# Layer 0 of a two-layer kernel: token buffers in two pairs, bias adds moved to block 3, no direct sums in block 6, the first block's own pieces in one step

## The chip, the cores and the metric

The kernel runs on one core of one Trainium2 chip. The metric is device time in microseconds (us), the median of several runs. The profile is of one execution, taken by the hardware profiler. Its engines are PE (TensorE; PEld are its weight loads), DVE (VectorE), ACT (ScalarE), POOL (GpSimd) and SP (SyncE, which here issues most DMAs). L1421 is line 1421 of the kernel before.

## The reference, cut to what matters

Two layers work on 4096 tokens of 256 features, all in float32. Layer 0, which the change touches, is attention over all tokens:

```python
x = layernorm(h); q = x @ wq.T + bq + sym_emb            # h: 32 x 128 tokens, 256 features
Q, K, V = q @ wQ.T + bQ, h @ wK.T + bK, h @ wV.T + bV     # 8 heads of 32
scores = einsum(Q, K) / sqrt(32)
scores = where(t_key > t_query, -inf, scores)             # t: time of the token, 0..127
ctx = softmax(scores) @ V
h = h + alpha * (ctx @ out_w.T + out_b)
```

Layer 1 is attention in a window of 24 tokens and then eight experts of three matrices each, weighted by a router. The change leaves it as it is.

## The kernel before

Layer 0 works on **8 blocks** of 512 tokens, sorted by time, so that block b sees the keys of blocks 0 to b alone. The 8 heads are two groups of four. A **unit** (b, g) is one block of queries with one group of heads; it is cut into **steps**, one for each tile of 128 keys (4b + 3 steps for group 0, 4b + 2 for group 1; the last tiles of a unit, which are partly masked, share steps). 265 steps in all are issued one after the other by one Python loop (from L1576). For each engine this order is the program, since the schedule is written out by hand. In pass n of the loop:

- `scores` (L1330): PE multiplies queries and keys of step n. The first head goes to the PSUM tile `sa` (one buffer), the other three to `sb` (two buffers, pool `ps_b`). Projections and sums take their PSUM from `ps_b` too, through `banks`.
- `product` (L1421): PE adds the weights times the values of step n - 2 to `av`. When a unit ends here, `evacuate` (L1436) copies `av` out on ACT, between the two exponentials.
- `exps`: ACT takes the exponential of `sa` (L1343) and of `sb` (L1345) into a tile `pt` (five buffers). Where a step crosses the mask, POOL clears corners of `pt` by three memsets (L1357); DVE and PE read `pt` after these.
- `add` (L1371 to L1407): DVE adds the `pt` of step n - 1 to `acc`, two heads at a time. This is for the sum of each softmax row.
- `close_sums` (L1451): one pass after the last product of a unit, PE adds up `acc` over the key partitions. Steps listed in `direct` are left out by `add`, and their `pt` is summed by PE here. `direct` held one step of either unit of block 6 and two of either unit of block 7.
- `invert` and `scale` (L1490, L1503), five and eleven passes later: the sums go through DRAM by small DMAs (`r16`, `flat`, `rec`) and DVE multiplies `ctx` by the inverse.
- Between these, `prep(b + 1)` makes the next block's keys, values and queries in four pieces: transposes (L986), keys (L995), values (L1041), queries (L1014). The loop spreads `count` pieces evenly over the block's steps. In block 0, the pieces of `rest_of_first` go ahead of them: the values of block 0, then keys and queries of its group 1. The pieces of `output_weights` (block 2) and `expert_norms` (block 3) come behind `prep`; the latter issue the copy `bnT` on DVE (L1265) and the band mask `bandb` on POOL (from L1237).

Input tiles come by DMAs on SP's queue, in the order of issue: `load_x` (L946) loads a block sorted by time ("xg" for projections, "xs" for the statistics of the layer norm), and `load_tokens` (L898) loads a block in its plain order ("tokens"), for the residual sum in layer 1's first part. All take buffers of 512 KB from the pool `tok`: one ring of four, tag "xg". A buffer is handed on when its last reader is done. `send_rstd(b + 1)` (L974, L978) sends the next block's inverse deviations through DRAM into a tile `rb`; it is issued on SP at the second step of a block, ahead of tokens that are loaded at the third.

`with_bias(n)` (L906) adds the output bias `outb` (made in block 2) to token tile n, on POOL. Tiles 0 to 11 were done in layer 0, six in the second unit of block 5 and six in that of block 6; the rest later. POOL runs its instructions in order and waits only for data, so an add that is written in a step may run as soon as the instruction ahead of it on POOL is done.

Of the kernel before, what the change touches and what calls it, by code (L numbers as in the profile page):

```python
# [10 lines left out]
F32 = mybir.dt.float32  # L11
# [5 lines left out]
P = 128  # L17
# [806 lines left out]
def fast_kernel(ctx: ExitStack, tc: tile.TileContext, ins: dict, out: bass.AP, narrow):  # L824
    nc = tc.nc
    x = ins["x"]
    _, N, T, D = x.shape
# [5 lines left out]
    NBLK = NT // BLK  # L833
    TPB = BLK // P
    HG = P // HD
    NGRP = H // HG
# [8 lines left out]
    def row(ap):  # L845
        return ap.rearrange("(o d) -> o d", o=1)
# [43 lines left out]
        nc.gpsimd.memset(big_t[:, :, z : z + SIDE], 0.0)  # L890


    tok = ctx.enter_context(tc.tile_pool(name="tok", bufs=4))
    held_tokens = {}

    def load_tokens(b, t):
        held_tokens[b] = t
        nc.sync.dma_start(  # L898
            out=t, in_=x[0, b * TPB : (b + 1) * TPB].rearrange("n t d -> t n d")
        )  # L900

    def tokens(n):
        return held_tokens[n // TPB][:, n % TPB, :]

    def with_bias(n):
        nc.gpsimd.tensor_tensor(tokens(n), tokens(n), outb, op=ALU.add)  # L906
# [21 lines left out]
    with ExitStack() as l0:  # L928
# [7 lines left out]
        rblk = {}  # L936

        def load_x(b, name, amid=()):
            xg = tok.tile([P, TPB, D], F32, tag="xg", name=f"{name}{b}")
            for tl in range(TT):  # L940
                if tl < len(amid):
                    amid[tl]()
                src = x[0][:, b * TPB * TT : (b + 1) * TPB * TT, :].rearrange(
                    "n (i tl) d -> tl n i d", tl=TT
                )[tl]
                nc.sync.dma_start(out=xg[tl * N : (tl + 1) * N], in_=src)  # L946
            return xg
# [140 lines left out]
        with tc.tile_pool(name="pw", bufs=1) as pw, tc.tile_pool(  # L1088
            name="ptr", bufs=8, space=PSUM
# [112 lines left out]

        def output_weights(banks):

            wo_n = tok.tile([P, TPB, D], F32, tag="xg", name="wo_n")[:, :2, :]
            nc.sync.dma_start(
                out=wo_n, in_=ins["L0_conv_out_w"].rearrange("(c p) d -> p c d", p=P)
            )
            nc.sync.dma_start(out=alpha, in_=row(ins["L0_conv_alpha"]).to_broadcast([P, 1]))
            nc.sync.dma_start(out=outb, in_=row(ins["L0_conv_out_b"]).to_broadcast([P, D]))  # L1210
            bvb = px.tile([P, 2, P], F32, tag="bvb", name="bvb", bufs=1)
            for c in range(2):
                nc.vector.tensor_copy(bvb[:, c, :], colT[:, c, 6:7].to_broadcast([P, P]))
            yield
            pss = banks("ps_wo", 2)
            for c in range(2):
                for k in range(2):
                    nc.tensor.transpose(
                        pss[c][:, k * P : (k + 1) * P], wo_n[:, k, c * P : (c + 1) * P], ident
                    )  # L1220
            for c in range(2):
                nc.scalar.copy(woT[:, c, :], pss[c][:, :D])
            nc.vector.tensor_scalar(woT, woT, alpha, None, op0=ALU.mult)
            yield
            ps = banks("ps_ob", 1)[0][:, :D]
            for c in range(2):
                nc.tensor.matmul(
                    ps, lhsT=bvb[:, c, :], rhs=woT[:, c, :], start=(c == 0), stop=(c == 1)
                )
            nc.vector.scalar_tensor_tensor(  # L1230
                out=outb, in0=outb, scalar=alpha, in1=ps, op0=ALU.mult, op1=ALU.add
            )
            yield
# [36 lines left out]
        with ExitStack() as at:  # L1270
# [29 lines left out]
            units = {(b, g): unit_steps(b, g) for b in range(NBLK) for g in range(NGRP)}  # L1300
            steps = [(b, g, k) for (b, g), unit in units.items() for k in range(len(unit))]

            direct = {u: () for u in units}
            for b, count in ((NBLK - 2, 1), (NBLK - 1, 2)):
                last = len(units[b, 0]) - 1
                direct[b, 0] = tuple(range(last - 1, last - 1 + count))
                last = len(units[b, 1]) - 1
                direct[b, 1] = tuple(range(last + 1 - count, last + 1))

            def carried(b, g):  # L1310

# [127 lines left out]
            FIRST = 3 * TPB  # L1439
# [96 lines left out]
            for n in range(10):  # L1536
                count = 3 if n < 4 else 2
# [19 lines left out]
            def rest_of_first():  # L1557
                pss = banks("psv0", 2)
                for f in [project_v(0, i2, hT0, pss[i2], True) for i2 in range(TPB // 2)]:
                    f()  # L1560
                yield
                for g in range(1, NGRP):
                    pss = banks(f"pskq0_{g}", 2)
                    copies = (
                        project_k(0, g, hT0, pss[0], True),
                        project_q(0, g, hT0, pss[1], later=True),
                    )
                    for f in copies:
                        f()
                    yield  # L1570


            u, z = NBLK - 3, NBLK - 2
            tokens_at = [(u, 0, 2), (u, 0, 4), (u, 1, 0), (z, 1, 0)]
            todo, done, count = iter(()), 0, 0
            later = {}  # L1576
            for n in range(len(steps) + LAG + 1 + 16):
                if n < len(steps):
                    b, g, k = steps[n]
                    own = sum(len(units[b, i]) for i in range(NGRP))  # L1580
                    if g == 0 and k == 0:
                        for _ in todo:
                            pass
                        todo, done, count = iter(()), 0, 5
                        if b + 1 < NBLK:
                            todo = prep(b + 1, banks)
                            if not b:
                                send_rstd(1)
                        if b == 0:
                            todo, count = itertools.chain(rest_of_first(), todo), 8  # L1590
                        if b == 2:
                            more = output_weights(banks)
                            next(more)
                            todo, count = itertools.chain(todo, more), 7
                        if b == 3:
                            more = expert_norms(banks)
                            next(more)
                            todo, count = itertools.chain(todo, more), 6
                        if 2 <= b < NBLK - 2:
                            xblk[b + 2] = load_x(b + 2, "xg")  # L1600
                    scores(b, g, k)
# [23 lines left out]
                if n < len(steps):  # L1625
                    at_step = g * len(units[b, 0]) + k + 1
                    closing = any(f is close_sums for f, _ in later.get(n, []))
                    if due == 2:
                        invert_rstd()
                        due = 0  # L1630
                    while done < count * at_step // own and not (closing and b):
                        if due == 1:

                            root_rstd()
                            due = 2
                        next(todo, None)
                        done += 1
                    if (b, g, k) in tokens_at:
                        nb = tokens_at.index((b, g, k))
                        load_tokens(  # L1640
                            nb, tok.tile([P, TPB, D], F32, tag="xg", name=f"tokens{nb}")
                        )
                    if n in load_at:
                        for lb in load_at[n][1:]:
                            got = xstat if load_at[n][0] == "xs" else xblk
                            got[lb] = load_x(lb, load_at[n][0])
                    for sb_, si in stat_at.get(n, ()):
                        stats(sb_, si, xstat[sb_])
                        if (sb_, si) == (NBLK - 1, TPB - 1):
                            cols = slice(2 * TPB, NTILE)  # L1650
                            nc.vector.tensor_scalar(
                                rstd0[:, cols], mean0[:, cols, 1], 1e-5, None, op0=ALU.add
                            )
                            due = 1
                    if 1 < b < NBLK - 1 and not g and k == 1:
                        send_rstd(b + 1)
                    if NBLK - 3 <= b < NBLK - 1 and g and 4 <= k < 4 + FIRST // 2:
                        with_bias((b - NBLK + 3) * FIRST // 2 + k - 4)
                for f, u in later.pop(n, []):
                    f(*u)  # L1660

# [838 lines left out]
    for name, cost, f, needs in jobs:  # L2500
        own = isinstance(name, tuple) and isinstance(name[1], int)
        b = name[1] if own else 2
        if own and name[0] in ("project", "normalise", "turn"):
            b = max(1, (b - 1) // TPB)
# [47 lines left out]
    for k in range(len(work)):  # L2552
# [7 lines left out]
        if k + 1 < len(work):  # L2560
            nb = work[k + 1][0]
# [23 lines left out]
        if one:  # L2585
            name = f"th{k + 1}"
# [55 lines left out]
```

## Time and profile before

| what | us |
|---|---|
| median of 3 runs (lowest, highest) | 1478.73 (1478.14, 1479.79) |
| profiled execution | 1477.89 |
| its span | 1476.1 |
| layer 0's steps, first to last exponential | 19.64 to 694.67 |
| block 3, unit 0 / unit 1, from | 155.03 / 196.68 |
| block 5, unit 1, from | 381.32 |
| block 6, unit 0 / unit 1, from | 436.05 / 499.42 |
| block 7, unit 0 / unit 1, from | 563.46 / 630.53 |

A unit starts here where ACT starts its first exponential. Granted clock of PE: 1.00 in all these stretches.

A row of the timeline has the start, the busy time of the merged instructions, engine, line, operation, tile written and tiles read, shape, count, and in brackets how long the engine stood idle before and what ended that. SPq rows are DMAs being issued, not transferred. A row of groups has count, busy time and mean. Idle time of an engine costs time only if the engine is the bound there, or if one that is waits for it.

### The profile page before, as it was taken

What the parts mean: (1) busy time and instruction counts of PE and PEld (TensorE: products, weight loads), DVE (VectorE), ACT (ScalarE), POOL (GpSimd) and SP (SyncE); (2) the same over time, 40 slices, a digit from 0 to 9 for tenths busy, and PEclk for the clock granted to TensorE, in tenths of its full rate; (3) what the DMA queues carried; (4) which work ended last, traced back from release to release, by engine and by line L of the source; (5) the groups of instructions that cost most, each with busy time, mean ns of one, the idle gap of its engine ahead of it and who ended that gap; (6) DMA issues with size and microseconds to landing.
All of it is one profiled execution on the core that took longest, in us unless ns stands there. A gap on an engine that the chain in (4) does not pass through costs nothing.

```text
span 1476.1 us, 23637 instructions
## 1 busy us (share of the span) xinstructions
PE 1454.4 (99%) x8873; PEld 842.4 (57%) x8873; DVE 1198.8 (81%) x2189; ACT 936.6 (63%) x1357; POOL 153.1 (10%) x318
## 2 busy tenths in 40 slices
PE   9999999999999999999899999999999999999998
PEld 6433232322322322222567888888888888888887
DVE  4778989899999999999647777777777778777775
ACT  4777878888889889988464445445445544444443
POOL 2211011000200200000163013020011000000000
PEclk9999999999999999999999999999999999999999
DMA  6220101021000000000332333433334344334442
GB/s 137 52 56 9 40 1 37 1 44 38 2 15 23 1 9 9 1 9 20 101 134 96 110 120 123 132 121 110 122 111 127 116 127 130 108 122 127 130 150 67
DMA packets 96377, 110.15 MB, mean 75 GB/s; under 512 B 17949, under 2 KB 85232, under 8 KB 96256
## 3 DMA queue, kind: packets, MB, share of 16 engines
q1 hardware_dynamic: 93280, 106.87, 24.3%
q8 instruction: 72, 1.18, 0.3%
q0 software_dynamic: 1888, 0.91, 0.2%
q10 hardware_dynamic: 1088, 0.79, 0.2%
q14 instruction: 49, 0.40, 0.1%
HBM read 98.87 MB, written 8.53 MB: 73 GB/s over the span
## 4 chain that ended last, share of the span: by engine, by line
PE 82%; DVE 10%; issue 3%; ACT 3%; DMA 1%; SPq 0%; DVEq 0%; POOL 0%; ACTq 0%; POOLq 0%
PE psh L2082 22%; PE sa L1330 14%; PE av L1421 14%; PE psy L2148 13%; DVE acc L1407 3%; PE psv L1041 2%; PE psk L995 2%; PE psq L1014 2%; PE psk L1831 2%; PE sums L1451 1%; PE sb L1330 1%; ACT h L2065 1%; PE psh L2087 1%; PE pso L1516 1%; PE pss L1843 1%
## 5 line engine op out<-in xcount | busy, mean ns | idle before, releaser
L1407 DVE TENSOR_TENSOR acc<-acc,pt 128x1024 f32<-128x1024 f32 (+2 forms) x470 | 517.7, 1167 | 22.0 <-POOL pt L1357 11.1
L1345 ACT ACTIVATE pt<-sb 128x1536 f32<-128x1536 f32 (+1 forms) x265 | 382.8, 1445 | 3.0 <-PE sb L1330 2.9
L1330 PE MATMUL sb<-q,kT 32*128 32x512 f32 (+3 forms) x1728 | 299.8, 600 | 0.5 <-DVE bnT L1265 0.5
L1330 PE MATMUL sa<-q,kT 32*128 32x512 f32 (+3 forms) x576 | 296.5, 600 | 1.9 <-ACT pt L1343 0.7
L2065 ACT ACTIVATE h<-h,bshift,bscale 128x256 f32<-128x256 f32 x244 | 159.2, 699 | 214.4 <-DVE h L2124 214.3
L1421 PE MATMUL av<-pt,v 128*32 128x512 f32 (+3 forms) x2304 | 281.4, 568 | 0.6
L2148 PE MATMUL psy<-wo,h 128*128 128x256 f32 x1024 | 243.6, 381 | 0.0
L2148 PEld LDWEIGHTS psy<-wo,h 128*128 128x128 f32 x1024 | 191.5, 190 | 31.0 <-issue 5.5
L1330 PEld LDWEIGHTS sa<-q,kT 32*128 32x128 f32 x576 | 85.8, 183 | 205.8 <-ACT pt L1343 171.6
L1343 ACT ACTIVATE pt<-sa 128x512 f32<-128x512 f32 (+1 forms) x265 | 157.8, 595 | 63.1 <-PE sb L1330 29.1
L1421 PEld LDWEIGHTS av<-pt,v 128*32 128x32 f32 x2304 | 47.8, 108 | 198.5 <-issue 175.5
L2156 DVE SCALAR_TENSOR_TENSOR tokens<-psy,w,tokens 128x256 f32<-128x256 f32 x256 | 111.2, 475 | 30.3 <-PE psy L2148 29.9
L2109 DVE TENSOR_TENSOR u<-psh,u 128x256 f32<-128x256 f32 x122 | 51.2, 420 | 98.2 <-ACT u L2108 97.7
L1357 POOL MEMSET pt<- 32x256 f32 (+4 forms) x123 | 52.2, 424 | 609.1 <-ACT pt L1345 508.1
L2065 ACT ACTIVATE h<-psh,bshift,bscale 128x256 f32<-128x256 f32 (+1 forms) x132 | 75.8, 576 | 50.8 <-PE psh L2082 43.5
L1330 PEld LDWEIGHTS sb<-q,kT 32*128 32x128 f32 x1728 | 90.1, 183 | 7.3 <-ACT pt L1345 4.3
L2108 ACT COPY u<-psh 128x256 f32<-128x256 f32 x122 | 43.9, 360 | 76.8 <-PE psh L2082 76.7
L2082 PE MATMUL psh<-tx,s 128*128 128x256 f32 x366 | 89.1, 379 | 0.3 <-DVE tx L2055 0.3
L2082 PE MATMUL psh<-th,s 128*128 128x256 f32 x366 | 89.0, 379 | 0.0
L2124 DVE TENSOR_TENSOR h<-psh,u 128x512 f32<-128x512 f32 x122 | 83.1, 681 | 4.2 <-PE psh L2082 4.0
L2082 PEld LDWEIGHTS psh<-tx,s 128*128 128x128 f32 x366 | 69.4, 190 | 10.2 <-DVE tx L2055 0.7
L2082 PEld LDWEIGHTS psh<-th,s 128*128 128x128 f32 x366 | 69.5, 190 | 9.6 <-DVE h L2124 0.2
(343 smaller groups left out, 1768.2 us busy)
## 6 DMA issues: line engine op xcount, KB each, us to landing
w<-in_L_ffn_W_dram SPq DMA_DIRECT2D x128, 256.0 KB
s<-kept SPq DMA_DIRECT2D x56, 512.0 KB
wo<-in_L_ffn_Wo_dram SPq DMA_DIRECT2D x64, 256.0 KB
xg<-in_x_dram SPq DMA_DIRECT2D x32, 128.0 KB
tokens<-in_x_dram SPq DMA_DIRECT2D x8, 512.0 KB
kept<-s SPq DMA_DIRECT2D x8, 512.0 KB
out_dram<-tokens SPq DMA_DIRECT2D x32, 128.0 KB
rec<-flat SPq DMA_DIRECT2D x60, 64.0 KB
```

What stands on the lines that cost most here:

```text
L1330: nc.tensor.matmul((sb[:, h - 1, :] if h else sa)[:, at : at + w], lhsT=kT[rows, gg, j * P : (j + 1) * P], rhs=q[rows, gg, lo : lo + w], s ...
L1343: nc.scalar.activation(pt[:, 0, used], sa[:, used], AF.Exp, scale=SCALE)
L1345: nc.scalar.activation(pt[:, 1:, used], sb[:, :, used], AF.Exp, scale=SCALE)
L1357: nc.gpsimd.memset(rows, 0.0)
L1407: nc.vector.tensor_tensor(acc[:, hs, cols], acc[:, hs, cols], pt[:, hs, at : at + w], op=ALU.add,)
L1421: nc.tensor.matmul(av[h * HD : (h + 1) * HD, lo : lo + w], lhsT=v[:, j, (g * HG + h) * HD : (g * HG + h + 1) * HD], rhs=pt[:, h, at : at + w],
L2065: nc.scalar.activation(dst, src, AF.Relu, bias=bshift[:, m, k : k + 1], scale=bscale[:, m, k : k + 1])
L2082: nc.tensor.matmul(ps, lhsT=w, rhs=x, start=start, stop=True, skip_group_check=True)
L2109: nc.vector.tensor_tensor(u, a[:, 1], u, op=ALU.add)
L2124: nc.vector.tensor_tensor(flat.rearrange("p (k c) -> p k c", k=2), self.q, self.u.unsqueeze(1).to_broadcast([P, 2, HB]), op=ALU.add,)
L2148: nc.tensor.matmul(pss[i], lhsT=ht[:, c, r * P : (r + 1) * P], rhs=wo[k][:, c, :], start=(c == 0), stop=(c == 1),)
L2156: nc.vector.scalar_tensor_tensor(out=tokens(n), in0=pss[i], scalar=w[:, r, e : e + 1], in1=tokens(n), op0=ALU.mult, op1=ALU.add,)
```

## The change

The four buffers become two pairs, "xa" and "xb". `xs` of blocks 2, 3, 6, 7 and `xg` of block 4, `wo_n` and tokens 0 and 1 take "xb", the others "xa". Tokens 0 and 1 are loaded in block 3 (third and tenth step of unit 0), not in block 5. `with_bias` runs for tiles 0 to 3 in unit 0 and 4 to 7 in unit 1 of block 3, and for tiles 8 to 11 in unit 1 of block 5; block 6 has none. `direct` names steps of block 7 alone. In block 0, the values and the keys and queries of group 1 are one piece, and 6 pieces are spread in place of 8.

```diff
-    tok = ctx.enter_context(tc.tile_pool(name="tok", bufs=4))
+    tok = ctx.enter_context(tc.tile_pool(name="tok", bufs=2))
...
-            xg = tok.tile([P, TPB, D], F32, tag="xg", name=f"{name}{b}")
+            late = b in ((2, 3, 6, 7) if name == "xs" else (4,))
+            xg = tok.tile([P, TPB, D], F32, tag="xb" if late else "xa", name=f"{name}{b}")
...
-            wo_n = tok.tile([P, TPB, D], F32, tag="xg", name="wo_n")[:, :2, :]
+            wo_n = tok.tile([P, TPB, D], F32, tag="xb", name="wo_n")[:, :2, :]
...
-            for b, count in ((NBLK - 2, 1), (NBLK - 1, 2)):
-                last = len(units[b, 0]) - 1
-                direct[b, 0] = tuple(range(last - 1, last - 1 + count))
-                last = len(units[b, 1]) - 1
-                direct[b, 1] = tuple(range(last + 1 - count, last + 1))
+            for g in range(NGRP):
+                last = len(units[NBLK - 1, g]) - 1
+                direct[NBLK - 1, g] = (last - 1, last)
...
                 for f in [project_v(0, i2, hT0, pss[i2], True) for i2 in range(TPB // 2)]:
                     f()
-                yield
                 for g in range(1, NGRP):
...
-            u, z = NBLK - 3, NBLK - 2
-            tokens_at = [(u, 0, 2), (u, 0, 4), (u, 1, 0), (z, 1, 0)]
+            tokens_at = [(3, 0, 2), (3, 0, 9), (NBLK - 3, 1, 0), (NBLK - 2, 1, 0)]
...
-                            todo, count = itertools.chain(rest_of_first(), todo), 8
+                            todo, count = itertools.chain(rest_of_first(), todo), 6
...
+                        tag = "xb" if nb < 2 else "xa"
                         load_tokens(
-                            nb, tok.tile([P, TPB, D], F32, tag="xg", name=f"tokens{nb}")
+                            nb, tok.tile([P, TPB, D], F32, tag=tag, name=f"tokens{nb}")
                         )
...
-                    if NBLK - 3 <= b < NBLK - 1 and g and 4 <= k < 4 + FIRST // 2:
-                        with_bias((b - NBLK + 3) * FIRST // 2 + k - 4)
+                    if (b, g) == (3, 0) and 5 <= k < 5 + TPB:
+                        with_bias(k - 5)
+                    if (b, g) == (3, 1) and 8 <= k < 8 + TPB:
+                        with_bias(TPB + k - 8)
+                    if b == NBLK - 3 and g and 6 <= k < 6 + FIRST - 2 * TPB:
+                        with_bias(2 * TPB + k - 6)
```

On POOL this puts the adds of tiles 0 and 1 between the last memset of block 2 and the first memset of block 3 (step 7 of unit 0), those of tiles 2 and 3 behind the latter, that of tile 4 behind the memset of step 7 of unit 1 and ahead of the band mask, and those of tiles 5 to 7 behind the mask.

## Prediction

> **What bounds the kernel now.** I read the page first (busy time, chain, groups), then layer 0 block by block as stretches, then the timeline at each place that the diff touches. The page:
>
> ```profile
> PE 1454.4 (99%) x8873; PEld 842.4 (57%) x8873; DVE 1198.8 (81%) x2189; ACT 936.6 (63%) x1357; POOL 153.1 (10%) x318
> ...
> PE 82%; DVE 10%; issue 3%; ACT 3%; DMA 1%; SPq 0%; DVEq 0%; POOL 0%; ACTq 0%; POOLq 0%
> ```
>
> TensorE (PE) is busy 99% and makes 82% of the chain; the granted clock is 1.00 in every stretch I asked for. So an edit counts only where it takes work from PE, or makes PE stand still. Block 3 is 155.03 to 233.88 us (PE busy 41.34 of 41.65 and 36.62 of 37.20), block 6 is 436.05 to 563.46 (62.69 of 63.37, 63.94 of 64.04). DVE is close behind: 62.84 of 63.37 in the first half of block 6. A step costs PE 2.07 us (scores 1.07, products 1.00), ACT 2.05 (0.60 + 1.45) and DVE 2.33 (two adds of 1.167); PE's extra work at projections lets DVE catch up.
>
> **Part 1, token loads and bias adds in block 3.** The order of issue shows one new dependence that matters. On POOL, the bias adds of tiles 0 and 1 now stand in front of the memset of block 3's first diagonal step (3,0,7). They wait for the load of tokens 0, and SP issues that load behind rb4. The trace of before at that place:
>
> ```profile
> 169.80 0.35 SPq L978 DMA_DIRECT2D rb<-rstd  x1
> 170.25 2.42 SPq L1482 DMA_DIRECT2D r<-ssb  x4
> ...
> 174.90 1.63 POOL L1357 MEMSET pt<- 32x256 f32 x3 [18.99 <-ACT pt L1345]
> ...
> 176.56 6.15 DVE L1407 TENSOR_TENSOR acc<-acc,pt 128x768 f32<-128x768 f32 x6 [1.03 <-POOL pt L1357]
> ...
> 176.90 1.07 PE L1421 MATMUL av<-pt,v 128*32 128x384 f32 x16
> ```
>
> The memset ends at 176.53; DVE starts on it at once, and PE 0.37 later, when its scores are through. There is no more cover than that 0.37. When does tokens 0 land? SP is free for it at 170.25. The same pair of transfers stands in block 5, rb issued at 316.65 and tokens right behind it:
>
> ```profile
> 317.10 0.38 SPq L898 DMA_DIRECT2D tokens<-in_x_dram  x1
> ...
> GB/s 0 0 0 0 0 0 0 25 41 66 0 0 0 0 0 74 156 139 139 172 139 180 106 119 262 336 266 254 246 229 152 8 20 25 20 25 12 0 0 0
> ```
>
> (the last line: 316 to 326 us in slices of 0.25). There the last bytes moved at 325.2, 8.1 us after the issue and 2.7 after rb's (322.4 by the packets). A load with nothing ahead of it took 3.5 (issued 461.60, bytes until 465.1). In block 3 rb4's packets end at 174.15; plus 2.7 gives 176.9, which I take; the ends are 170.25 + 3.5 = 173.75 and 170.25 + 8.1 = 178.3. Two bias adds with DVE standing still take 0.73 each (median of L906). So the memset starts at 176.9 + 0.1 + 1.46 = 178.5 and ends 1.63 later at 180.1; PE starts at 180.2 instead of 176.90: **+3.3 us**. Ends: a landing at 173.75 puts the adds beside DVE's (1.18 each) and gives +1.1; 178.3 gives +4.7. Behind the waiting add on POOL stands only this memset; DVE's add waits for it, and so does PE's product, behind which stand block 4's key projection (3.7 us) and everything after. ACT may run on but PE, not ACT, bounds here (ACT 33.70 of 41.65), so nothing is caught up. SP's r, flat and rec transfers also move back: DVE's reciprocal at 175.28 would wait for r until some 177.5, covered by the longer wait for the memset. Tokens 1 follows rec (after 180); nothing on SP is due behind it until 204.02, and its reader comes at 220.
>
> Tiles 2 and 3 follow the memset, tile 4 stands ahead of the band-mask instructions (220.52), tiles 5 to 7 behind them. What such an add does to DVE is seen in block 5:
>
> ```profile
> 383.01 8.49 POOL L906 TENSOR_TENSOR tokens<-tokens,outb 128x256 f32<-128x256 f32 x6
> ...
> 386.39 2.25 DVE L1383 TENSOR_TENSOR acc<-pt,pt 128x512 f32<-128x512 f32 x2 [0.73 <-ACT pt L1345]
> ```
>
> Two DVE adds that take 0.69 each elsewhere (median of L1383) take 2.25 here, 1.12 each, and the next two (L1388, median 0.69) 2.35: about +0.54 us of DVE for each POOL add, and POOL's own go from 0.73 to 1.18. [...] For tiles 2 and 3 (1.1) DVE has waits of 0.92 and 2.34 soon after (184.77, 198.65): nothing. For tile 4 it has none, since PE itself waits for DVE there:
>
> ```profile
> 226.16 0.32 DVE L1265 COPY bnT<-psbn 128x160 f32<-128x160 f32 x1
> ...
> 226.53 1.13 PE L1330 MATMUL sb<-q,kT 32*128 32x512 f32 x6 [0.49 <-DVE bnT L1265]
> ```
>
> DVE runs without a gap from 211.44 to that copy, so tile 4's 0.54, and as much again if tile 5 begins before the copy, lengthen PE's 0.49. I take **+0.8** (0 if POOL is the one held off, as in its first 3.25 us add; 1.7 for three adds). The rest of DVE's lag meets block 3's last sums at 239.39, where PE's next scores wait for ACT until 241.21 anyway: **+0.1** (0 to 0.5).
>
> What leaves blocks 5 and 6 frees DVE by 2 and 6 times 0.54. At 397.08 DVE waits 1.08 for ACT, at 517.29 it waits 1.27: it was ahead in both, so the gain is a longer wait: 0. The swapped buffer rings change no other wait: xg7 takes xg5's place, read a block earlier.
>
> **Part 2, no direct sums in block 6.** PE loses two times eight matmul records (about 0.9 us each until the next issue, 504.54 to 505.40 and 568.93 to 569.82); DVE gains two times two adds, 2.33 each. Is PE's next work ready earlier? At the second join:
>
> ```profile
> 569.26 1.45 ACT L1345 ACTIVATE pt<-sb 128x1536 f32<-128x1536 f32 x1
> ...
> 569.82 1.04 PE L1451 MATMUL sums<-acc,ones 128*32 128x512 f32 x8
> ...
> 570.79 0.70 PE L1330 MATMUL sb<-q,kT 32*128 32x512 f32 x3
> ```
>
> The sb scores need the bank that ACT's exponential frees at 570.71. Without direct sums they still start at 570.79. Blocks 3 to 4 have no direct sums and show the wait: sums 239.39, sa 240.39, sb 241.21 after an exponential ending at 241.15, products 1.06 after sb in both. The first join is alike (exponential ends 506.29, sb 506.38). So **0**; a gain of up to 1.9 stays as an end. On DVE, the first join's 2.03 us wait for POOL (501.07) takes all but 0.3 of the added 2.33; the second's 1.83 (568.91) all but 0.5, and 0.37 of that goes into the wait at 573.92. The 0.13 left runs through block 7, where DVE has no gap from 573.92 to 638 and ACT does wait for it (0.35 at 628.00, 0.59 at 630.53): **+0.1** (0 to 0.6).
>
> **Part 3, first block.** Same matmuls, other order. Before, PE stood 0.68 for hT (31.46). After: values 19.54 to 23.18, keys and queries to 26.83, scores to 27.97, then the transposes wait for DVE's q (kT copy, then q, until 28.34), and the third scores' sb part waits for the second exponential (28.5 to 29.95). Products 30.7, keys 31.7, next scores 35.3 against 35.09: **+0.2** (-0.5 if the new waits are covered, +0.6).
>
> **Sum.** 3.3 + 0.8 + 0.1 + 0 + 0.1 + 0.2 = +4.5 us. The profiled execution took 1477.89 (span 1476.1, 1.79 around it): 1482.4. The median of the runs is 1478.73, 0.84 more: **1483.2**. About 0.2% (3 us) is what can be told from no change.
>
> **Rivals.**
> A, the forecast, +2.5 to +6.5: 63%.
> B, tokens 0 lands before 173.6, so that both adds end ahead of the memset's due time: no stall, the rest +1.2 (0 to 2.5), 1479.9. For it: loads alone moved at up to 389 GB/s; against: rb4 is still moving at 174. 17%, all within 0.2%.
> C, not slower: PE's sums really go. Mechanism: with POOL's adds gone, ACT and DVE come earlier to the joins, so sb is free and PE saves 1.9; the first block's 0.68 goes too, and 0.6 that PE waits for DVE at block 5's last sums: -3.2, 1475.5, if also B holds. It decides if the exponential before sb ends 0.9 earlier; ACT runs from 502.11 to 506.29 almost without a gap, which speaks against. 8%, faster.
> D, the wait is longer (landing at 178 or later, DVE's lag passed on): +6.5 to +10, 1486.5. 12%.
> A's low part (8%) also falls within 0.2%: faster 0.08, same 0.25, slower 0.67. The range leaves out C and D's upper half: 1478.4 to 1486.8 (the upper bounds sum to +8.1).
>
> **What would show it.** Right: in block 3, POOL's first bias add starts near 177 after a DMA wait, the memset behind it ends near 180, PE's product has a gap of 3 us there; bnT's copy and the sb behind it are later by 0.5 to 1; the joins at 506 and 570 show PE waiting for ACT, sb to products unchanged; block 6 as long as before. Wrong: the memset still ends 1.6 us after its exponential, or block 6 is 2 us shorter.

## The result, and the profile after

The changed kernel takes 1483.93 us (median of 7 runs, 1482.42 to 1485.15), the kernel before, run beside it, 1479.79 (7 runs, 1478.14 to 1481.34): a ratio of 1.0031, 95% interval 1.0021 to 1.0041. A second set of runs of the same kernel gave 1482.99 against 1479.77, 1.0029 (1.0020 to 1.0038). So the change makes the kernel slower by some 0.3%, and a median of 1483.2 was forecast. The profiled execution took 1483.93 (span 1482.1), 6.04 more than the profiled one of before.

The page of the kernel after, the busy times and the chain's shares, shows next to nothing of it:

```profile
PE 1456.1 (98%) x8857; PEld 844.9 (57%) x8857; DVE 1201.8 (81%) x2193; ACT 936.7 (63%) x1357; POOL 154.8 (10%) x318
...
PE 83%; DVE 10%; ACT 3%; issue 3%; DMA 0%; POOL 0%; ACTq 0%; DVEq 0%
```

PE went from 99% to 98% with 16 matmuls fewer, and was still 1.7 us longer busy. That is the first hint: a matmul somewhere takes longer than it did.

To find where, each trace was cut into units at the first exponential on `sa` of every unit (block, half); a unit's length is from there to the next unit's. Against before, the unit (3,0) is 46.32 in place of 41.65 (+4.67), (3,1) 37.54 for 37.19 (+0.35), (4,0) 46.61 for 46.27 (+0.34), (7,0) 66.66 for 67.07 (-0.41), (7,1) 64.42 for 64.13 (+0.29). The first exponential comes 0.41 later and layer 1 is 0.47 longer, where no code differs. All the others are within 0.05, and together they make the 6.0 by which the spans differ.

The timeline of the kernel after, from the load of tokens 0 on (start, busy time, engine, line, operation, tiles, count, idle time before and its releaser), at the place that the prediction quoted of before:

```profile
170.98 0.38 SPq L898 DMA_DIRECT2D tokens<-in_x_dram  x1
...
177.33 1.41 POOL L906 TENSOR_TENSOR tokens<-tokens,outb 128x256 f32<-128x256 f32 x2 [21.05 <-issue]
...
178.80 1.63 POOL L1356 MEMSET pt<- 32x256 f32 x3
180.46 8.23 DVE L1406 TENSOR_TENSOR acc<-acc,pt 128x768 f32<-128x768 f32 x7 [2.36 <-POOL pt L1356]
...
180.48 1.93 PE L1420 MATMUL av<-pt,v 128*32 128x384 f32 x16 [3.14 <-POOL pt L1356]
...
182.34 4.30 PE L996 MATMUL psk<-hT,wKT 128*128 128x512 f32 x8
```

The two bias adds wait for the load (the row says "issue", but the tokens' last packets end at 176.61, and the adds start 0.7 later), the memset for the adds, and PE for the memset: 3.14 us. That is the predicted chain, almost to the tenth. But the rows behind the gap are longer than those of before: the product's 16 matmuls take 1.93 us, and the key projection 4.30 for 3.70 in before:

```profile
177.91 3.70 PE L995 MATMUL psk<-hT,wKT 128*128 128x512 f32 x8
```

From the product's start to the next scores it is 6.09 us (180.48 to 186.57), in before 4.63 (176.90 to 181.53). The stretches of 3.4 us around the gap in the kernel after tell why (length, busy time and count of PE, PEld, DVE, ACT and POOL, then PEclk, the granted clock):

```profile
core 0: us, PE busy (x) PEld busy (x) DVE busy (x) ACT busy (x) POOL busy (x), PEclk, DMA share, GB/s
...
176.80:180.20 3.40, 0.54 (x8) 0.00 (x0) 0.25 (x1) 2.37 (x3) 2.73 (x5) 1.00 0.03 2
180.20:183.60 3.40, 3.12 (x18) 1.34 (x19) 3.10 (x3) 0.00 (x0) 3.12 (x3) 0.50 0.43 118
183.60:187.00 3.40, 3.40 (x11) 1.33 (x14) 3.30 (x4) 0.32 (x1) 0.00 (x0) 1.00 0.34 118
```

PE worked 0.54 of the 3.40 us, and in the next 3.41 (180.17 to 183.59 in the clock's record) it was granted half its clock. The gap cost twice: 3.21 of waiting (the product starts 25.08 after the unit's start, in before 21.87) and 1.46 of slow matmuls.

The smaller terms, in the same timeline further on (tile 4's add ahead of the band mask; `bnT` and the scores behind it; the last sums of block 3):

```profile
225.52 1.10 POOL L906 TENSOR_TENSOR tokens<-tokens,outb 128x256 f32<-128x256 f32 x1
...
231.55 0.31 DVE L1266 COPY bnT<-psbn 128x160 f32<-128x160 f32 x1
...
231.91 1.13 PE L1329 MATMUL sb<-q,kT 32*128 32x512 f32 x6 [0.84 <-DVE bnT L1266]
...
244.89 2.10 PE L1450 MATMUL sums<-acc,ones 128*32 128x512 f32 x8 [0.37 <-DVE acc L1406]
```

PE waits 0.84 for `bnT`, in before 0.49. And the last sums of block 3, which in before waited for ACT (0.22) and then took 1.06, now wait for DVE, which arrives late with `acc`, and are spread over 2.10. The row of before:

```profile
239.39 1.06 PE L1451 MATMUL sums<-acc,ones 128*32 128x512 f32 x8 [0.22 <-ACT pt L1345]
```

The second join of block 6 (the last sums, ACT's exponential, the next block's scores):

```profile
574.67 1.50 PE L1450 MATMUL sums<-acc,ones 128*32 128x512 f32 x8 [0.22 <-ACT pt L1344]
...
574.99 1.45 ACT L1344 ACTIVATE pt<-sb 128x1536 f32<-128x1536 f32 x1
...
576.49 0.70 PE L1329 MATMUL sb<-q,kT 32*128 32x512 f32 x3
```

The direct sums are gone, and `sb` still waits for the bank that the exponential frees at 576.44. Block 6's units are 63.37 and 64.07, against 63.37 and 64.03 in before.

### The profile page after: what moved, and what is told of

Its sections match the earlier page's. It is cut to its first block, busy times and chain, and to the rows that moved or that the text cites. A ratio compares the mean times of both kernels' runs of the same rounds, so it can differ in the third digit from the quotient of the medians.

```text
span 1482.1 us, 23622 instructions
## 1 busy us (share of the span) xinstructions
PE 1456.1 (98%) x8857; PEld 844.9 (57%) x8857; DVE 1201.8 (81%) x2193; ACT 936.7 (63%) x1357; POOL 154.8 (10%) x318
## 4 chain that ended last, share of the span: by engine, by line
PE 83%; DVE 10%; ACT 3%; issue 3%; DMA 0%; POOL 0%; ACTq 0%; DVEq 0%
PE psh L2084 22%; PE sa L1329 15%; PE av L1420 14%; PE psy L2150 13%; DVE acc L1406 3%; PE psv L1042 2%; PE psk L996 2%; PE psk L1833 2%; PE psq L1015 2%; PE sums L1450 2%; PE sb L1329 1%; ACT h L2067 1%; PE psh L2089 1%; PE pso L1515 1%; PE pss L1845 1%
## 5 line engine op out<-in xcount | busy, mean ns | idle before, releaser
L1406 DVE TENSOR_TENSOR acc<-acc,pt 128x1024 f32<-128x1024 f32 (+2 forms) x474 | 523.9, 1175 | 23.8 <-ACT pt L1344 12.2
```

The lines of the kernel that those rows point to most:

```text
L1406: nc.vector.tensor_tensor(acc[:, hs, cols], acc[:, hs, cols], pt[:, hs, at : at + w], op=ALU.add,)
```

## The experiments

The theory, T: the loss is the memset that waits behind adds that wait for a load; PE's gap costs by itself, and then by the clock; adds beside a DVE without gaps cost the rest; the direct sums and the first block cost nothing. The rivals: the bias adds cost wherever they stand, since POOL and DVE hold each other up (R); another part of the change carries the loss; the matmuls behind the gap are slow for another reason than the clock.

The table has all runs. "Delay" is the start of the product of (3,0,7), counted from the unit's start, less before's 21.87. "Rest" is the length of (3,0), less before's 41.65 and less the delay. "Clock" is the time at a clock of 0.5 in (3,0) by the clock's record.

| kernel | delay | rest | clock | (3,0) | (3,1) | (4,0) | median us | ratio (95%) |
|---|---|---|---|---|---|---|---|---|
| before | 0 | 0 | 0 | 41.65 | 37.19 | 46.27 | 1479.79 | |
| after | 3.21 | 1.46 | 3.41 | 46.32 | 37.54 | 46.61 | 1483.93 | 1.0031 (1.0021, 1.0041) |
| after, again | 3.14 | 0.00 | 0 | 44.79 | 37.54 | 46.59 | 1482.99 | 1.0029 (1.0020, 1.0038) |
| adds behind memset | 0.02 | -0.01 | 0 | 41.66 | 37.54 | 46.61 | 1480.55 | 1.0006 (0.9997, 1.0015) |
| token part alone | 2.24 | 0.00 | 0 | 43.89 | 37.54 | 46.62 | 1482.90 | 1.0030 (1.0018, 1.0042) |
| sums part alone | 0.00 | 0.00 | 0 | 41.65 | 37.21 | 46.27 | 1478.89 | 0.9999 (0.9990, 1.0008) |
| first-block part alone | 0.00 | 0.00 | 0 | 41.65 | 37.20 | 46.27 | 1478.49 | 0.9999 (0.9990, 1.0008) |
| load first | 1.42 | 0.00 | 0 | 43.07 | 37.55 | 46.60 | 1481.31 | 1.0015 (1.0006, 1.0024) |
| PE kept busy | 2.54 | 0.00 | 0 | 44.19 | 37.54 | 46.60 | 1482.95 | 1.0028 (1.0017, 1.0039) |
| one add ahead | 2.34 | 1.64 | 3.41 | 45.63 | 37.54 | 46.62 | 1483.29 | 1.0029 (1.0017, 1.0041) |
| four adds ahead | 4.03 | 2.83 | 6.83 | 48.51 | 37.56 | 46.59 | 1485.07 | 1.0035 (1.0021, 1.0049) |
| all behind | 0.01 | -0.01 | 0 | 41.65 | 39.32 | 46.28 | 1479.85 | 1.0005 (0.9996, 1.0014) |
| adds in DVE's gaps | 0.01 | 0.00 | 0 | 41.66 | 37.21 | 46.29 | 1479.04 | 0.9997 (0.9988, 1.0006) |

The delays and the rests are of one profiled execution each, the medians and ratios of all runs, each against before on its own chip.

### The four adds behind the memset

```diff
-                    if (b, g) == (3, 0) and 5 <= k < 5 + TPB:
-                        with_bias(k - 5)
+                    if (b, g) == (3, 0) and 8 <= k < 8 + TPB:
+                        with_bias(k - 8)
```

> The changed kernel with the four bias adds of block 3's first half put behind the memset of step (3,0,7) in POOL's order; all else stays. Theory T (the loss is the memset that waits behind adds that wait for the load of tokens 0; PE's gap there, 3.14 us, and the 3.41 us at a granted clock of 0.5 that follow it): the memset ends near 176.5, PE's gap before the product is 0.4 or less, the clock stays 1.0, the unit (3,0) falls from 46.32 to 41.7 (before: 41.65), and the time is some 4.6 below the changed kernel: about 1479.3. Rival R (the adds cost because POOL's and DVE's work on SBUF hold each other up, wherever they stand): (3,0) stays above 44 and the time at 1482 or more.

The timeline of this kernel at the same place:

```profile
174.84 1.63 POOL L1356 MEMSET pt<- 32x256 f32 x3 [19.01 <-ACT pt L1344]
...
176.54 4.67 POOL L906 TENSOR_TENSOR tokens<-tokens,outb 128x256 f32<-128x256 f32 x4
...
176.84 1.07 PE L1420 MATMUL av<-pt,v 128*32 128x384 f32 x16
177.84 3.70 PE L996 MATMUL psk<-hT,wKT 128*128 128x512 f32 x8
```

The memset waits for its exponential and for nothing else, the product starts on time, the key projection is back at 3.70, and (3,0) at 41.66. The same four adds run beside DVE's adds and cost nothing here. R falls: the place in POOL's order is what costs. The median, 1480.55, is above the 1479.3 of the expectation, which missed there. 0.69 of it is left in (3,1) and (4,0). A drop of the clock elsewhere may add to it: this trace has one of 3.41 us at 838.32, in layer 1, and its layer 1 is 783.5 long, in before 781.4.

### Each part by itself

The token part alone, on the kernel before (with the tags of `xg` and `wo_n` and the two later lines of `with_bias` as in the change):

```diff
-    tok = ctx.enter_context(tc.tile_pool(name="tok", bufs=4))
+    tok = ctx.enter_context(tc.tile_pool(name="tok", bufs=2))
...
-            tokens_at = [(u, 0, 2), (u, 0, 4), (u, 1, 0), (z, 1, 0)]
+            tokens_at = [(3, 0, 2), (3, 0, 9), (NBLK - 3, 1, 0), (NBLK - 2, 1, 0)]
...
+                    if (b, g) == (3, 0) and 5 <= k < 5 + TPB:
+                        with_bias(k - 5)
```

> The kernel before with the token part alone: two pairs of buffers, the loads at (3,0,2) and (3,0,9), the bias adds in block 3; direct sums and first block as before. Theory T: all of the loss is in this part, so (3,0) is 46.3, (3,1) 37.5, (4,0) 46.6, and the time is 5.0 to 5.4 above before's: 1484.5 (more than the changed kernel by the 0.1 to 0.5 that its other two parts may have gained). Rival S (the direct sums or the first block carry a part of the loss): 1482 or less.

The sums part alone:

```diff
-            for b, count in ((NBLK - 2, 1), (NBLK - 1, 2)):
-                last = len(units[b, 0]) - 1
-                direct[b, 0] = tuple(range(last - 1, last - 1 + count))
-                last = len(units[b, 1]) - 1
-                direct[b, 1] = tuple(range(last + 1 - count, last + 1))
+            for g in range(NGRP):
+                last = len(units[NBLK - 1, g]) - 1
+                direct[NBLK - 1, g] = (last - 1, last)
```

> The kernel before with the direct sums of block 6 taken away, nothing else. Theory T: the scores of the next block wait for the bank that ACT's exponential frees, with or without the sums, so both units of block 6 keep their length (63.37 and 64.03), DVE carries a little into block 7, and the time is 0.0 to +0.4 from before's 1479.8. Rival C (PE's sums really go): -2 to -4, 1476 to 1478.

The first-block part alone:

```diff
-                yield
...
-                            todo, count = itertools.chain(rest_of_first(), todo), 8
+                            todo, count = itertools.chain(rest_of_first(), todo), 6
```

> The kernel before with the first block's own pieces in one step (one yield less, six steps instead of eight), nothing else. Theory T: (0,0) stays at 16.7 within 0.1, and the time is within 0.3 of before's 1479.8. Rival: the order makes later units of block 0 or 1 longer or shorter and the time moves by 0.5 or more to either side.

The token part has the whole loss by the times: 1.0030, where the whole change has 1.0031 and 1.0029; the two others have 0.9999 each. With the sums part, block 6 stays at 63.36 and 64.03, and block 7 gets 0.38 shorter in its first unit and 0.63 longer in the second, +0.25 in all. With the first-block part, (0,0) is 16.66 for 16.71.

The token part alone missed its expectation in the trace: (3,0) is 43.89, not 46.3. Two things are different there. POOL's first add starts 20.96 after the unit's start, in the changed kernel 21.93, since SP issued the load earlier (169.63, 14.51 after the unit's start, for 15.58). And the clock does not drop. The trace is of the fastest of this kernel's six runs (1481.16 to 1486.05). The rows of this kernel, product and key projection, and then its stretches:

```profile
179.23 1.07 PE L1422 MATMUL av<-pt,v 128*32 128x384 f32 x16 [2.17 <-POOL pt L1358]
...
180.23 3.70 PE L996 MATMUL psk<-hT,wKT 128*128 128x512 f32 x8
```

```profile
174.10:177.50 3.40, 2.96 (x24) 0.53 (x20) 1.57 (x3) 3.19 (x4) 1.41 (x2) 1.00 0.24 73
177.50:180.90 3.40, 1.67 (x18) 0.85 (x19) 1.69 (x2) 1.51 (x2) 3.19 (x5) 1.00 0.26 75
180.90:184.30 3.40, 3.40 (x12) 1.32 (x14) 3.26 (x4) 0.33 (x1) 1.25 (x1) 1.00 0.57 163
```

### How much of the gap: one add ahead, four adds ahead

```diff
-                    if (b, g) == (3, 0) and 5 <= k < 5 + TPB:
-                        with_bias(k - 5)
+                    if (b, g) == (3, 0) and k in (6, 8, 9, 10):
+                        with_bias((6, 8, 9, 10).index(k))
```

> The changed kernel with the bias add of tile 0 alone ahead of the memset of (3,0,7), the three others behind it. The memset then waits for the same load but for one add less: it ends 0.7 earlier, PE's gap is 2.4 instead of 3.14. Theory T: if the shorter gap leaves the clock at 1.0, (3,0) is 41.65 + 2.5 = 44.1 and the time 2.2 below the changed kernel, 1481.7; if it does not, 45.6 and 1483.2. Rival R: the number of adds counts, not their place: 46.3.

```diff
-                    if (b, g) == (3, 0) and 5 <= k < 5 + TPB:
-                        with_bias(k - 5)
+                    if (b, g) == (3, 0) and 3 <= k < 3 + TPB:
+                        with_bias(k - 3)
```

> The changed kernel with all four bias adds of block 3's first half ahead of the memset of (3,0,7) in POOL's order, at the steps 3 to 6. Theory T (each add ahead of the memset is one more 0.73 us in which PE stands): the memset ends 1.46 later against the tokens' landing, PE's gap is 4.0 to 4.7 instead of 3.14, with the clock's drop (6.8 us at 0.5 if two stretches of 3.413 are hit) (3,0) is 47 to 49.5, and the time 1 to 3 above the changed kernel: 1485 to 1487. Rival (PE's gap is set by the load alone, the adds run in its shadow): 46.3, and the changed kernel's time.

With four adds ahead, the timeline shows the chain stretched:

```profile
176.64 2.78 POOL L906 TENSOR_TENSOR tokens<-tokens,outb 128x256 f32<-128x256 f32 x4 [20.51 <-issue]
...
181.16 1.94 PE L1420 MATMUL av<-pt,v 128*32 128x384 f32 x16 [3.96 <-POOL pt L1356]
...
183.02 5.67 PE L996 MATMUL psk<-hT,wKT 128*128 128x512 f32 x8
```

From POOL's first add to the product it is 4.52 us, with two adds ahead 3.15 (180.48 - 177.33), with one 2.46 (179.63 - 177.17): 0.69 us for each add ahead. So the load sets when the chain begins, and every add ahead lengthens it. The gap of 3.96 is a little below the 4.0 to 4.7 expected, because the load came 0.55 earlier against the unit's start than in the changed kernel. The clock is at 0.5 for 6.83 us, twice 3.41, and the rest is 2.83. With one add ahead, the gap is 2.26 and the clock drops all the same:

```profile
176.80:180.20 3.40, 1.14 (x16) 0.29 (x12) 0.84 (x2) 2.40 (x3) 2.82 (x5) 1.00 0.03 2
180.20:183.60 3.40, 3.40 (x15) 1.40 (x8) 3.26 (x4) 0.00 (x0) 3.40 (x3) 0.50 0.45 89
```

So the clock dropped with a gap of 2.26 us, and not with one of 2.17 (the token part alone). Gaps so nearly alike make it doubtful that the length decides; the second run of the changed kernel, below, settles this.

### The clock: PE kept busy, and the changed kernel once more

Fourteen transposes that nothing reads, ahead of the product of (3,0,7):

```diff
+                    if steps[n - LAG] == (3, 0, 7):
+                        idle = banks("idle", 1)[0]
+                        for _ in range(14):
+                            nc.tensor.transpose(idle[:, :P], ident, ident)
```

> The changed kernel with 14 transposes of the identity into a bank that nothing reads, put in PE's order ahead of the product of (3,0,7): PE works through the wait for the memset. Theory T (the second half of the loss is the granted clock, 0.5 for 3.41 us after a gap of 3.14 us): the product still starts near 180.5, but the clock stays 1.0, the key projection behind it takes 3.70 instead of 4.30 us and the product 1.5 instead of 1.93, (3,0) falls from 46.32 to about 44.9, and the time by 1.4: 1482.5. Rival U (the matmuls behind the gap are slow for another reason, as POOL's adds of tiles 2 and 3 in SBUF beside them): they stay at 4.30 and 1.93, (3,0) at 46.3, and the time at the changed kernel's or above.

```profile
177.21 1.75 PE L1606 MATMUL idle<-ident 128*128 128x128 f32 x14
...
179.72 1.07 PE L1420 MATMUL av<-pt,v 128*32 128x384 f32 x16 [0.77 <-POOL pt L1356]
...
180.72 3.70 PE L996 MATMUL psk<-hT,wKT 128*128 128x512 f32 x8
```

The product still comes 2.54 late, POOL's adds of tiles 2 and 3 run beside it as in the changed kernel, and the matmuls have their old length: the rest is 0.00. So it is not POOL's traffic that made them slow. What speaks for the work on PE having kept the clock is the stretch of 3.413 us from 177.13 to 180.54 (why this stretch, the next run shows): the whole wait lies in it, as in the first trace of the changed kernel, and PE was busy for 2.64 us of it, 1.75 of these with the transposes. Without them some 0.9 would be left (an estimate), and stretches with 0.54 and 1.14 lost the clock. The median, 1482.95, is 0.98 below the changed kernel's first median and level with its second; the expected 1.4 is not clear of that spread.

The changed kernel, unedited:

> The changed kernel once more, nothing edited. So far a drop of the granted clock to 0.5 began in each trace that had one at a whole number of 3.413 us after the clock's first record, and lasted 3.413. Theory W (the clock is judged in such fixed stretches, whose place against the kernel differs from run to run): a drop, if there is one in block 3, begins again on that grid, between 177.3 and 183 us, and the unit (3,0) is 44.2 to 45.0 without it, 45.6 to 46.6 with it; the time is 1482.4 to 1485.2 as in the runs so far, in steps of some 1.5. Rival (the drop begins a fixed time after the gap's start): it begins some 2.9 us after PE stops, off the grid.

```profile
177.32 1.41 POOL L906 TENSOR_TENSOR tokens<-tokens,outb 128x256 f32<-128x256 f32 x2 [20.99 <-issue]
...
180.47 1.07 PE L1420 MATMUL av<-pt,v 128*32 128x384 f32 x16 [3.08 <-POOL pt L1356]
...
181.47 3.70 PE L996 MATMUL psk<-hT,wKT 128*128 128x512 f32 x8
```

This is the same gap within 0.06 us, at the same place, and no drop: the length of the gap is not what decides. From the product to the next scores it takes 4.63 (180.47 to 185.10), as in before; (3,0) is 44.79. In this trace the clock's record starts at 4.59, in the first one at 6.09. Steps of 3.413 us (the length of the first trace's drop) counted from there have a border at 178.67 here, in the middle of the gap, and in the first trace at 176.76 and 180.17, about its two ends. The stretches on this trace's grid:

```profile
175.25:178.66 3.41, 2.14 (x20) 0.47 (x16) 0.73 (x2) 3.20 (x5) 1.34 (x2) 1.00 0.31 99
178.66:182.08 3.42, 1.61 (x18) 0.79 (x19) 1.63 (x2) 0.69 (x1) 3.21 (x6) 1.00 0.25 71
182.08:185.49 3.41, 3.41 (x12) 1.38 (x14) 3.27 (x4) 0.28 (x1) 1.31 (x1) 1.00 0.40 122
```

Here the grid cuts the gap in two, and PE was busy for 2.14 and 1.61 us of the two steps; both kept the clock. In the first trace nearly the whole gap fell into one step (0.54 busy), with one add ahead likewise (1.14), and the step after it ran at 0.5. With the token part alone it was cut again (1.67 at the least), and the clock stayed. All drops in these traces, in block 3 and elsewhere, begin at a whole number of 3.413 us after the clock's first record (in the first trace 51 of them, from 6.09 to 180.17), and those of block 3 and layer 1 last one or two such steps (3.41 or 6.83). The rival, a drop at a fixed time after the gap's start, would have dropped the clock here too.

This bears on the medians. Whether the drop comes differs from run to run, and in the two profiled executions of the changed kernel it went with the place of the grid: 1483.93 with the drop (borders at 176.76 and 180.17) and 1482.47 without (178.67), a difference of 1.46. For the other runs the record has the mean granted clock, in steps of 0.001, which is some 3 us at half the clock. Of the 74 runs of before that stand beside the experiments, 33 have a mean of 0.998 or less, and their median is 1479.93; that of the other 41 is 1478.32. Of the changed kernel's 18 runs, 15 have 0.998 or less, with a median of 1483.16; the other three took 1481.48 to 1482.62. So before loses clock too in part of its runs. Where in a run it was lost, the mean does not say (it also counts the end of the run, where the clock falls to 0.5 from 1474.84 on in before's trace and from 1480.65 in the changed kernel's first), so in how many runs the gap of block 3 cost the clock stays open.

### The load first

```diff
-            tokens_at = [(3, 0, 2), (3, 0, 9), (NBLK - 3, 1, 0), (NBLK - 2, 1, 0)]
+            tokens_at = [(3, 0, 0), (3, 0, 9), (NBLK - 3, 1, 0), (NBLK - 2, 1, 0)]
```

> The changed kernel with the load of tokens 0 issued two steps earlier, at (3,0,0), where SP sends it ahead of rstd and rb of block 4; the bias adds stay ahead of the memset on POOL. Theory T (the adds cost because their data is not there): the tokens land near 165, the two adds run beside DVE and end before the memset's due time of 174.9, PE's gap and the clock of 0.5 go, (3,0) is 41.7 to 42.7, and the time is 4 to 5 below the changed kernel, about 1479.5. Rival R (the place ahead of the memset is bad by itself, or POOL's adds beside DVE's are): (3,0) 44 or more, 1482 or more. If rb of block 4 lands later behind the load and DVE or PE waits for it instead, (3,0) is long too, but with the wait at another instruction.

```profile
162.25 0.40 SPq L898 DMA_DIRECT2D tokens<-in_x_dram  x1
...
166.78 9.20 DVE L1406 TENSOR_TENSOR acc<-acc,pt 128x1024 f32<-128x1024 f32 x8
...
171.78 5.47 POOL L906 TENSOR_TENSOR tokens<-tokens,outb 128x256 f32<-128x256 f32 x2 [15.21 <-DMA tokens<-in_x_dram]
...
177.31 1.63 POOL L1356 MEMSET pt<- 32x256 f32 x3
...
178.99 1.07 PE L1420 MATMUL av<-pt,v 128*32 128x384 f32 x16 [1.35 <-POOL pt L1356]
```

The loss halves (1.0015), but does not go: (3,0) is 43.07, above the 42.7 that T allowed. The adds now begin 5.85 earlier against the unit's start (16.08 for 21.93), 3.8 ahead of the memset's due time (its exponential is through at 175.55). But the first takes 4.79 us, where the second takes 0.72: it starts in the middle of eight DVE adds without a pause (166.78 to 175.98) and ends at 176.56, 0.6 after the last of them. The memset then starts at 177.31 in place of 175.6. So here R is half right: by these times, an add that stands ahead of the memset costs by DVE too, not by DVE's delay but by its own. DVE's adds went on beside it at their usual length (9.20 for the eight, 1.15 each; 1.167 in before). Why POOL's add lasted until they were through, the runs do not show. The add began only at 171.78, with the tokens' last data packets at 166.4, because the load was signalled late: the trace has its sixteen completion signals between 165.69 and 171.61, in the changed kernel between 175.92 and 177.03, with the last packets at 176.61. Why they lag by 5.2 us here and by 0.4 there is not settled; here the transfer of the inverse deviations (`rstd`) was issued right behind the load, and its own signals came until 171.85.

### The last four adds

All adds behind both memsets, the second four behind the band mask of (3,1):

```diff
-                    if (b, g) == (3, 0) and 5 <= k < 5 + TPB:
-                        with_bias(k - 5)
-                    if (b, g) == (3, 1) and 8 <= k < 8 + TPB:
-                        with_bias(TPB + k - 8)
+                    if (b, g) == (3, 0) and 8 <= k < 8 + TPB:
+                        with_bias(k - 8)
+                    if (b, g) == (3, 1) and 9 <= k < 9 + TPB:
+                        with_bias(TPB + k - 9)
```

> The changed kernel with block 3's adds behind both memsets: tiles 0 to 3 behind that of step (3,0,7), tiles 4 to 7 behind the band mask of (3,1,8). Theory T: (3,0) 41.7, (3,1) back from 37.54 to 37.2, (4,0) 46.3 to 46.6, the time 0.3 below the kernel with only the first four moved, about 1479.2, so within 0.2% of before. Rival R: beside DVE the adds cost the same anywhere, (3,1) or (4,0) stays longer than before by 0.3 or more each.

```profile
224.43 6.68 POOL L906 TENSOR_TENSOR tokens<-tokens,outb 128x256 f32<-128x256 f32 x4
...
227.48 1.84 PE L1329 MATMUL sb<-q,kT 32*128 32x512 f32 x6 [1.02 <-DVE bnT L1266]
```

T missed here: (3,1) gets longer, 39.32, not back to 37.2. The adds run right where DVE works towards `bnT` (copied at 227.12), PE's wait for it is 1.02 in place of 0.84, and the clock drops to 0.5 for 3.41 us from 227.77, on the grid again. Only (4,0) is back at 46.28: its last sums of block 3 wait 0.21 for ACT, as in before, and DVE itself waits 0.62 there, which fits a PE so late that DVE caught up. The place among POOL's instructions was not the cause of these two terms, then, but the place in DVE's time.

The last four at the first four steps of (3,1), where DVE waits anyway:

```diff
-                    if (b, g) == (3, 0) and 5 <= k < 5 + TPB:
-                        with_bias(k - 5)
-                    if (b, g) == (3, 1) and 8 <= k < 8 + TPB:
-                        with_bias(TPB + k - 8)
+                    if (b, g) == (3, 0) and 8 <= k < 8 + TPB:
+                        with_bias(k - 8)
+                    if (b, g) == (3, 1) and k < TPB:
+                        with_bias(TPB + k)
```

> The changed kernel with the first four bias adds of block 3 behind the memset of (3,0,7) and the other four at the first four steps of (3,1), where DVE in the kernel before waits three times (2.34 us ahead of 198.65, 1.78 ahead of 201.72, 2.67 ahead of 211.44). Theory T (what is left with the first four adds moved, +0.35 in (3,1) and +0.34 in (4,0), comes from adds that stand beside a DVE without gaps): (3,0) 41.65, (3,1) 37.2, (4,0) 46.27, all as before, and the time within 0.5 of before's. Rival R (the adds beside DVE cost the same wherever they are, or the bias adds of tiles 4 to 7 are not the cause): (3,1) and (4,0) together stay 0.6 or more above before, and the time 0.8 or more.

```profile
195.48 6.67 POOL L906 TENSOR_TENSOR tokens<-tokens,outb 128x256 f32<-128x256 f32 x4
...
227.30 1.13 PE L1329 MATMUL sb<-q,kT 32*128 32x512 f32 x6 [0.49 <-DVE bnT L1266]
```

PE's wait for `bnT` is 0.49, as in before, and all three units have before's length within 0.02. With this, the changed kernel, its buffers, loads, sums and first block included, is at 0.9997 (0.9988 to 1.0006): no different from before. By the units' lengths, the loss was wholly where eight adds stood in POOL's order and in DVE's time. No run pointed to a version faster than before.

## Why the prediction was right, and where it was not

**The mechanism and the sign held.** The chain of load, adds, memset and product was found from the order of issue and priced at +3.3; it measured +3.21 and +3.14 in the two traces of the changed kernel. Its steps: landing taken as 176.9, adds from 177; measured 177.33 with a unit that starts 0.37 later. Memset's end 180.1; measured 180.43. With the adds moved, the term is 0.02. That it agrees to the tenth is in part luck. Two steps of it were off and cancel: with the 0.37 taken off, the tokens' last packets ended at 176.24 and not at 176.9 (1.63 behind those of rb4, not 2.7), but the adds began 0.72 after them and not 0.1. And the term itself varies: the two other traces with two adds ahead, the token part alone and the one with PE kept busy, have 2.24 and 2.54.

**The total held without the clock.** The prediction added 4.5 to the profiled 1477.89 and had 1482.4. The trace without a drop took 1482.47. But here too luck helped: the changed places of layer 0 make only 3.7 of its 4.6 (3.14 in (3,0), 0.35 in (3,1), 0.32 in (4,0), -0.11 in block 7, -0.04 in the first block), and 0.9 comes from a first exponential 0.47 later and a layer 1 that is 0.43 longer, where no code differs. The first trace, with the drop, is 1.46 above it, and that term is not in the sum. The step that failed is "PE starts at 180.2 instead of 176.90: +3.3 us", with its end of +4.7 for a late landing: it priced the gap as a wait alone. The clock had been read as 1.00 everywhere, and that it would stay so was taken for granted; but those stretches had no gap like the one forecast (PE was busy 41.34 of 41.65). That the medians agreed so well, 1483.2 with 1483.93 and 1482.99, is in part luck as well: against before's own median beside them they are 4.14 and 3.22 more, not 4.5. They mix runs with the drop and without, and before's own median went from 1478.73 in 3 runs to 1478.77 to 1479.79 in the later sets.

**Tile 4's add: +0.8 predicted, +0.35 measured.** The wait for `bnT` is the place, and the sign is right. Only one add stood beside DVE ahead of the copy, and DVE's five adds there took 0.36 more (5.52 for 5.16); the prediction's 0.54 for an add, and half as much again for the next, was too much. **The last sums of block 3: +0.1 predicted, +0.34 measured**: the scores waited no longer for ACT, as the prediction had it, but the sums themselves for DVE (0.37). The two errors, -0.45 and +0.24, partly cancel.

**The sums part: 0 for PE, as predicted**, and rival C (-3.2) did not happen: without direct sums the scores waited for the same exponential. What DVE carries into block 7 was +0.1; it measured -0.12 in the changed kernel and +0.25 with this part alone. **The first block: +0.2 predicted, -0.04 measured.**

**Rivals B and D.** B asked for a landing before 173.6; in the nine traces with the load at its place, the tokens' last packets ended between 175.3 and 177.0. D's price, +6.5 to +10, is reached in the trace of the kernel with four adds ahead (+6.86 in (3,0) alone), by more adds and the clock, not by a later landing; that kernel's median is 5.3 above before's.

## What to carry to other kernels

Before an instruction is put on an engine's queue, look at what stands behind it there: here two adds that waited for a load held three small memsets of 1.63 us in all behind them on POOL, and with them PE's product, which came 3.21 and 3.14 us late in the two traces of the changed kernel. Behind the memsets in the order, the same adds cost nothing (0.02). When PE is the bound, price a gap on PE twice, as the wait (3.21 here) and as the clock that may follow (1.46), and expect the second to come and go from run to run (1.46 in one trace of the changed kernel, 0.00 in the other). Put work that slows a busy engine into that engine's own waits: the same four adds cost 0.7 us beside a DVE without gaps and 0.0 in its gaps.

## What the runs showed of the hardware

- The granted clock fell to 0.5 for 3.413 us, or twice that, always on a grid of 3.413 us counted from the clock's first record; the place of the grid against the kernel differs from run to run (first record at 4.59 and 6.09 us in the two traces of the changed kernel). Steps of this grid with 0.54 and 1.14 us of PE work lost the clock, steps with 1.61 and 1.67 kept it in the token rows of block 3. This is not a rule: in the kernel with all adds behind, a step with PE busy for 2.39 us of it lost the clock (at 227.77), and in layer 1 a step with 1.97 us lost it in one trace (at 838.32, with the four adds behind the memset) and one with as much kept it in before (833.10 to 836.50). What the clock counts as work was not found out.
- A POOL add that started while DVE worked without a pause took 4.79 us in place of 0.72 (load first), and ended 0.6 us after DVE's last add of that row. Others beside DVE's adds took 1.1 to 1.7 us each (in the changed kernel one in 1.10 at 225.52 and two in 2.90 at 180.51; four in 6.68 with all adds behind).
- The same load was issued 14.5 to 15.6 us after its unit's start in the six traces with an add ahead of the memset, and POOL's first add began 20.96 to 21.93 after that start. A wait that hangs on it differs by 1 us among these kernels; the two traces of the changed kernel differ by 0.07.
- In these traces the end of a load's data was not its end for the engine that waited: the last completion signal came 0.4 us behind the last data packet in the changed kernel, and 5.2 us behind it with the load first.
